# Two graph layers on one core: the transform back in small pieces behind given instructions, GpSimd's sums in order of use, and the next group's first layers 0 at a group's end

## The chip, the core and the metric

The kernel runs on one core of a Trainium2 chip. The metric is the time of one execution in microseconds (us) on the device. The engines are TensorE (PE: matmuls; PEld is its loading of weights), VectorE (DVE), ScalarE (ACT), GpSimd (POOL) and SyncE (SP), which here only issues transfers. Each takes its own instructions in a fixed order, and waits where one of them needs another engine or a transfer. All data is float32.

## What is computed

64 graphs of 256 nodes with 256 features go through two layers. Cut to what matters:

```
# layer 0
norm_adj = d_inv_sqrt[:, :, None] * adjacency_matrix * d_inv_sqrt[:, None, :]
h = einsum('bnm,bmf->bnf', norm_adj + alpha * eye(N), x)
x = layernorm(x + h @ W.T + b)
# layer 1
h = relu(bn1(conv1(x)))                      # per node
x_conv = relu(bn2(conv2(h)) + x)             # 17 taps along the nodes
s = x @ w_se.T + b_se                        # 3 numbers a node
A = exp(-dist(s, s)) * mask                  # mask: ones
x_nmp = A @ relu(x @ w_msg.T + b_msg)
gi = concat([x_conv, x_nmp]) @ w_ih.T + b_ih
gh = x @ w_hh.T + b_hh
# r, z = sigmoid of thirds of gi + gh, nn = tanh(gi_n + r * gh_n)
x = layernorm(x + (1 - z) * nn + z * x)
```

## The kernel before, in words

**Groups and passes.** The convolution of 17 taps is done in the frequency domain: each graph's 256 nodes are cut into 8 tiles of 32, and the spectra of 16 graphs fill the 128 rows of a matmul. So the 64 graphs form 4 groups of Q = 16, and there is one pass q of the transform for each group. A pass has four kinds of work:

- **Layers**: `layer0(g)` (L326) and `layer1(g, V, place)` (L403) for each graph. Layer 1 writes the graph's spectrum into the big tile V (L460), and stores what the gate needs (x1_d, xn_d) to DRAM.
- **Products**: 12 steps (`products`, L528) multiply the spectra by the taps' spectra u, which come from DRAM in 71 loads of 256 KB a pass on SP's queue (`load_u`, L498, six buffers). The results go into M, which is the same memory as V.
- **The transform back**, on DVE alone, in place in M: `real_transform` and `complex_begin` run with the steps, `complex_end` (L692) after them. `output` (L679) makes two of the 32 nodes of each tile and stores them to xc_d on SP's queue.
- **Gates**: `gru(g)` (L767) for each graph of the group. It reads inputs (the transposed features), and four sums of them that GpSimd makes (`input_sums`, L758) for a Strassen-like product with 7 blocks instead of 8. xc is read from DRAM, x1 is added to it by a transfer of GpSimd's queue (`residual`, L737), and it is transposed on PE (`transposed`, L743).

**How passes overlap.** V and M are one tile, so the next group's layers can't write V while the transform back still reads M. The first AHEAD = 6 graphs of the next group write a second tile V2 instead, and four ACT copies (L998) move them to V when the transform has ended. The other 10 graphs follow, with the first EARLY = 4 gates of the group just transformed beside them. The other 12 gates ("late") run beside the next pass. The pools of the gate tiles (`gate`) and of V2 (`ahead`) are opened once, before pass 0.

**How the order is made.** Each function is a generator; a `yield` ends a piece. The program from L966 on weaves pieces: `take(stage, n)` runs n pieces, `merge(main, other, every)` puts one piece of other behind every so many of main, `chain` joins stages, `graphs` (L879) runs layer 1 of a graph with layer 0 of the graph two further on at the places of `PLACES`. The order written so is a priority, not yet the order on an engine. A planner that models the durations places the instructions of every engine: of those that it holds to be ready, it takes the one that was written first. So an instruction can be moved far ahead of its place in the text where its inputs are ready early and its engine is idle in the model. `tc.issue_after(i)` in a `with` forbids this: instructions of the block on i's engine are placed behind i. It adds no wait of its own. On the chip the order on each engine is then fixed.

**Names and lines of the changed places.** Instructions on DVE, most of which read what PE has just made: x1 in layer 0 (L396), h (L423), msg (L444), aT (L481, which reads what ACT made) in layer 1, and first (L793), trz (L800), gn (L822), y (L840) in a gate. GpSimd's sums: S[:,2] is L761, S[:,0] L762, S[:,1] L763, S[:,3] L764. S[:,0] and S[:,3] read the transposed convolution; S[:,2] reads only what the transfers of `load_gate` bring; S[:,1] reads S[:,0]. In a gate the blocks with S[:,0] and S[:,1] come first (p15, p26), those with S[:,2] and S[:,3] after them (p7, p34). The layer norm's power is taken on GpSimd too (L308), as is that of the degrees (L352).

Of the kernel before, what the change touches and what calls it, by code (L numbers as in the profile page):

```python
# [26 lines left out]
def kernel(  # L27
# [55 lines left out]
    def accbank(name):  # L83
        return psacc.tile([P, 512], F32, tag="acc", name=name)


# [242 lines left out]
    def layer0(g):  # L329
# [65 lines left out]
        for c in range(NCH):  # L395
            nc.vector.scalar_tensor_tensor(  # L396
                x1[:, c, :], p[:, c, :], dis[:, c : c + 1], x_t[:, c, :], op0=ALU.mult, op1=ALU.add
            )
# [4 lines left out]
    def layer1(g, V, place):  # L403
# [13 lines left out]
        for c in range(NCH):  # L417
            p = bank("p_conv1")[:, : D + NSE]
            for k in range(DCH):
                nc.tensor.matmul(  # L420
                    p, x1T[:, k, c * P : (c + 1) * P], wc1[:, k, :], start=k == 0, stop=k == DCH - 1
                )
            nc.vector.tensor_tensor(h[:, c, :], p, bc1, op=ALU.add)  # L423
        nc.scalar.activation(h[:, :, :D], h[:, :, :D], AF.Relu)  # L424
# [14 lines left out]
        for c in range(NCH):  # L439
            for k in range(DCH):  # L440
                nc.tensor.matmul(  # L441
                    p[:, c, :], x1T[:, k, c * P : (c + 1) * P], wmsg[:, k, :], start=k == 0, stop=k == DCH - 1
                )
        nc.vector.tensor_tensor(msg, p, bmsg_t.unsqueeze(1).to_broadcast([P, NCH, D]), op=ALU.add)  # L444
        nc.scalar.activation(msg, msg, AF.Relu)
# [30 lines left out]
        for c in range(NCH):  # L476
# [3 lines left out]
            nc.scalar.activation(aT[:, c].rearrange("p n q -> p (n q)"), p, AF.Exp, bias=nsq[:, c : c + 1], scale=2.0)  # L480
        nc.vector.tensor_mul(aT, aT, adjT[:, :, 0:3:2, :])  # L481
        yield
# [90 lines left out]
    def four(re, im):  # L573


        by = im - re
        sub2(blocks(re, by, 2), blocks(re + 2, by, 2))
        sub2(blocks(re, by), blocks(re + 1, by))
        add2(M[:, re + 2, :], M[:, im + 3, :])
        sub2(M[:, im + 2, :], M[:, re + 3, :])  # L580

# [30 lines left out]
    def real_transform():  # L612
# [12 lines left out]

        four(8, 12)
        yield
# [30 lines left out]
    def four_turned(re, im, angle):  # L658


        by, low = abs(re - im), min(re, im)
        z = [blocks(low + i, by) for i in range(4)]
        c2, t2 = turned(re + 2, im + 2, 2 * angle)
        stt(z[2], t2, -c2, z[0], op0=ALU.mult, op1=ALU.add)
        stt(z[0], t2, c2, z[0], op0=ALU.mult, op1=ALU.add)
        yield
        c1, t1 = turned(re + 1, im + 1, angle)
        c3, t3 = turned(re + 3, im + 3, 3 * angle)
        stt(z[3], t3, -c3 / c1, t1, op0=ALU.mult, op1=ALU.add)
        stt(t1, t3, c3 / c1, t1, op0=ALU.mult, op1=ALU.add)  # L670
        stt(z[1], t1, -c1, z[0], op0=ALU.mult, op1=ALU.add)
        stt(z[0], t1, c1, z[0], op0=ALU.mult, op1=ALU.add)
        yield
        for lo, hi, by in ((re + 2, im + 3, c1), (im + 2, re + 3, -c1)):
            stt(M[:, hi, :], M[:, hi, :], by, M[:, lo, :], op0=ALU.mult, op1=ALU.add)
            stt(M[:, lo, :], M[:, lo, :], 2.0, M[:, hi, :], op0=ALU.mult, op1=ALU.subtract)
        yield

    def output(q, n, re, im):  # L679


        plain = M[:, n // 8 * 8 + ORDER.index(n % 8), :]
        x, y = M[:, re, :], M[:, im, :]
        t = freq.tile([P, 2, D], F32, name="turn", bufs=3)
        by = [real_part(t[:, j, :], x, y, 2 * math.pi * (n + 16 * j) / FL) for j in range(2)]
        low = min(re, im)
        for j in range(2):
            stt(M[:, low + 16 * j, :], t[:, j, :], by[j], plain, op0=ALU.mult, op1=ALU.add)
        nc.sync.dma_start(
            xc_d[q].rearrange("g (t a b) d -> (g t) a b d", a=2, b=16)[:, :, n, :], M[:, low : low + 17 : 16, :]  # L690
        )

    def complex_end(q):

        four(CR, CI)
        yield
        for outs in (((0, 0, 0), (8, 1, 0)), ((4, 2, 0), (12, 3, 1))):
            for n, i, exchanged in outs:
                output(q, n, (CR, CI)[exchanged] + i, (CI, CR)[exchanged] + i)
            yield  # L700

        add2(M[:, CR + 4 : CR + 6, :], M[:, CI + 6 : CI + 8, :])
        sub2(M[:, CI + 4 : CI + 6, :], M[:, CR + 6 : CR + 8, :])
        yield
        for n, re, im, angle in ((2, CR + 4, CI + 4, math.pi / 4), (6, CI + 6, CR + 6, 3 * math.pi / 4)):
            low = min(re, im)
            c, t = turned(re + 1, im + 1, angle)
            stt(blocks(low + 1, 16), t, -c, blocks(low, 16), op0=ALU.mult, op1=ALU.add)
            stt(blocks(low, 16), t, c, blocks(low, 16), op0=ALU.mult, op1=ALU.add)
            yield  # L710
            output(q, n, re, im)
            output(q, n + 8, re + 1, im + 1)
            yield
        for n, re, im, angle in ((1, CR + 8, CI + 8, math.pi / 8), (3, CI + 12, CR + 12, 3 * math.pi / 8)):
            yield from four_turned(re, im, angle)
            output(q, n, re, im)
            output(q, n + 8, re + 1, im + 1)
            yield
            output(q, n + 4, re + 2, im + 2)
            output(q, n + 12, im + 3, re + 3)  # L720
            yield

# [35 lines left out]
    def input_sums(g):  # L758
        A11, A12, A21, A22 = halves(GATE[g][1])
        S = SUMS[g] = gate.tile([P, 4, HALF, P], F32, name="sums", bufs=1)  # L760
        nc.gpsimd.tensor_tensor(S[:, 2], A11, A21, op=ALU.subtract)  # L761
        nc.gpsimd.tensor_tensor(S[:, 0], A21, A22, op=ALU.add)  # L762
        nc.gpsimd.tensor_tensor(S[:, 1], S[:, 0], A11, op=ALU.subtract)  # L763
        nc.gpsimd.tensor_tensor(S[:, 3], A12, S[:, 1], op=ALU.subtract)  # L764

    def gru(g):
# [25 lines left out]
        first = gate.tile([P, 2, D], F32, name="first", tag="gn")  # L792
        nc.vector.tensor_add(first, half(p15), brz_t)  # L793
        nc.vector.tensor_add(trz[:, 0:2], first[:, 0:1].to_broadcast([P, 2, D]), half(p26))
# [4 lines left out]
        nc.vector.tensor_add(trz[:, 3], trz[:, 1], p7[:, :D])  # L799
        nc.vector.tensor_add(trz[:, 1:3], trz[:, 1:4:2], half(p34))  # L800

# [6 lines left out]
        for c in range(NCH):  # L808
# [12 lines left out]
            gn = gate.tile([P, 2, D], F32, name="gn")  # L821
            nc.vector.tensor_add(gn, p.rearrange("p (i d) -> p i d", i=2), bn_t)  # L822
            nc.vector.scalar_tensor_tensor(
# [15 lines left out]
            y, t, n = x1[:, part], trz[:, 1:4:2][:, part], nn[:, part]  # L839
            nc.vector.scalar_tensor_tensor(y, t, 3.0, y, op0=ALU.add, op1=ALU.mult)  # L840
            nc.vector.scalar_tensor_tensor(n, t, 1.0, n, op0=ALU.subtract, op1=ALU.mult)
# [30 lines left out]
    def run(stage):  # L872
        for _ in stage:
            pass


    PLACES = (("other",), ("layer0",), (), (), ("layer0",), ("other", "layer0"), ())

    def graphs(first, part, V, others):  # L879


        for i in part:
            load(first + i + 3)
            given = {"layer0": layer0(first + i + 2) if i + 2 < Q else iter(()), "other": others[i]}
            for piece, _ in enumerate(layer1(first + i, V, i)):
# [49 lines left out]
    ustream = ctx.enter_context(tc.tile_pool(name="ustream", bufs=6))  # L935
    gate = ctx.enter_context(tc.tile_pool(name="gate", bufs=2))
    ahead = ctx.enter_context(tc.tile_pool(name="ahead", bufs=1))


    AHEAD = 6  # L940
    V2 = ahead.tile([P, FL, DCH, AHEAD * GT], F32, name="V2")
    EARLY = 4

# [16 lines left out]
    def nothing():  # L960
        return iter(())

    late = nothing()
    for q in range(NQ):
# [3 lines left out]
        if more:  # L968
            if q:
                others = [both(take(late, 3 if i % 3 == 0 else 2), take(end, 2)) for i in range(AHEAD)]  # L970
            else:
                others = [nothing() for _ in range(AHEAD)]
            begin = chain(merge(layer0(first), layer0(first + 1)), graphs(first, range(AHEAD), V2, others))
        sums(0)
        real = real_transform()
        for step in range(STEPS):
# [5 lines left out]
            if q:  # L982
                run(take(late, (0, 1, 1, 1, 1, 1, 2, 1, 2, 1, 2, 1)[step]))
            else:
                run(take(begin, 2 + step // 4))
        run(real)
        if not q:
            run(merge(begin, end, 3))
        elif more:
            run(merge(merge(take(late, 20), take(begin, 6), 3), take(end, 5), 5))  # L990
            run(begin)
        else:
            run(merge(late, end, 2))
        if more:
            run(late)
            run(end)
            for f in range(0, FL, 12):
                nc.scalar.copy(V[:, f : f + 12, :, : AHEAD * GT], V2[:, f : f + 12])  # L998
            early = gates(q, range(EARLY))
            others = [take(early, 2) for _ in range(Q)]  # L1000
            run(graphs(first, range(AHEAD, Q), V, others))
            run(early)
            late = gates(q, range(EARLY, Q))
        else:
# [54 lines left out]
```

## Time and profile before

| | us |
|---|---|
| three runs | 2186.56, 2187.06, 2191.32 |
| profiled execution | 2186.0 |
| PE busy | 2067.5 (95%) |
| DVE busy | 1547.1 (71%) |
| ACT busy | 831.2 (38%) |
| POOL busy | 664.5 (30%) |

The stages follow each other so: layers of group 0 with the making of the taps' spectra up to about 288 us; pass 0's products from there to about 400 us, its transform back to 470 us; then layers of group 1 with gates to 640 us. Pass 1's products run to 760 us and its transform back ends at 884 us; layers with gates go on to 1160 us. Pass 2 does the same 520 us later. Pass 3's products start at 1680 us and its transform back ends at 1926 us; what is left are gates alone.

In the profile's view of 40 slices each digit is the busy share of an engine in a slice of 54.6 us, in tenths. PE's time while it waits between matmuls counts as idle, but the end of a matmul is modelled, so counts of matmuls in a stretch say more than busy time.

### The profile page before, as it was taken

What the parts mean: (1) busy time and instruction counts of PE and PEld (TensorE: products, weight loads), DVE (VectorE), ACT (ScalarE), POOL (GpSimd) and SP (SyncE); (2) the same over time, 40 slices, a digit from 0 to 9 for tenths busy, and PEclk for the clock granted to TensorE, in tenths of its full rate; (3) what the DMA queues carried; (4) which work ended last, traced back from release to release, by engine and by line L of the source; (5) the groups of instructions that cost most, each with busy time, mean ns of one, the idle gap of its engine ahead of it and who ended that gap; (6) DMA issues with size and microseconds to landing.
All of it is one profiled execution on the core that took longest, in us unless ns stands there. A gap on an engine that the chain in (4) does not pass through costs nothing.

```text
span 2186.0 us, 28897 instructions
## 1 busy us (share of the span) xinstructions
PE 2067.5 (95%) x9805; PEld 1750.7 (80%) x9805; DVE 1547.1 (71%) x3691; ACT 831.2 (38%) x1847; POOL 664.5 (30%) x640
## 2 busy tenths in 40 slices
PE   6999899969999988999999998899999999899998
PEld 5888778758888876888888887788888887778887
DVE  5555458875568799655557889855565879987766
ACT  3665533445531123455452122446543112222222
POOL 2445310122322233223231224322231223344442
PEclk9999999989999999999999999999999999999999
DMA  3765656443346644434336654433334654344441
GB/s 110 239 193 194 222 178 207 151 134 102 111 137 201 191 130 108 131 91 123 105 101 190 207 144 130 116 114 108 102 97 126 205 160 118 114 121 111 105 113 53
DMA packets 251331, 305.64 MB, mean 140 GB/s; under 512 B 18324, under 2 KB 229864, under 8 KB 251184
## 3 DMA queue, kind: packets, MB, share of 16 engines
q1 hardware_dynamic: 183680, 200.46, 30.0%
q10 hardware_dynamic: 44480, 67.39, 8.7%
q0 software_dynamic: 23024, 35.95, 8.2%
q8 instruction: 78, 1.28, 0.2%
q14 instruction: 69, 0.57, 0.1%
HBM read 200.62 MB, written 103.06 MB: 139 GB/s over the span
## 4 chain that ended last, share of the span: by engine, by line
PE 50%; DVE 14%; issue 6%; POOL 6%; ACT 4%; DMA 0%; ACTq 0%; POOLq 0%; SPq 0%; DVEq 0%
PE p_rz L780 18%; PE p_n L817 9%; PE p_k L510 8%; PE p_nmp L486 2%; PE p_out L392 2%; PE p_dft L455 2%; PE p_conv L420 2%; POOL sums L762 2%; PE p_hT L382 1%; PE p_msg L441 1%; POOL ln_rs L308 1%; POOL sums L764 1%; PE p_dist L479 1%; POOL sums L763 1%; DVE gn L822 1%
## 5 line engine op out<-in xcount | busy, mean ns | idle before, releaser
L780 PE MATMUL p_rz<-wrz,sums 128*128 128x256 f32 x1536 | 355.8, 383 | 19.4 <-DVE gn L822 9.8
L817 PE MATMUL p_n<-wn,inputs 128*128 128x256 f32 x1536 | 353.0, 383 | 16.2 <-DVE first L793 15.7
L780 PEld LDWEIGHTS p_rz<-wrz,sums 128*128 128x128 f32 x1536 | 288.4, 191 | 70.7 <-issue 15.8
L817 PEld LDWEIGHTS p_n<-wn,inputs 128*128 128x128 f32 x1536 | 286.6, 191 | 62.6 <-DVE first L793 19.0
L780 PE MATMUL p_rz<-wrz,inputs 128*128 128x256 f32 x1152 | 272.9, 380 | 2.4 <-ACT inputs L752 1.8
L308 POOL TENSOR_TENSOR ln_rs<-ln_rs,neg_half 128x2 f32<-128x2 f32 x129 | 100.2, 777 | 537.3 <-DVE ln_rs L307 451.5
L780 PEld LDWEIGHTS p_rz<-wrz,inputs 128*128 128x128 f32 x1152 | 216.7, 190 | 33.9 <-ACT inputs L752 3.8
L352 POOL TENSOR_TENSOR dis<-deg,neg_half 128x2 f32<-128x2 f32 x64 | 48.6, 760 | 425.1 <-DVE deg L350 320.4
L829 ACT ACTIVATE nn<-gn 128x256 f32<-128x256 f32 x128 | 53.2, 416 | 326.0 <-DVE gn L826 325.5
L510 PE MATMUL p_k<-u,VM 128*128 128x256 f32 x736 | 175.1, 380 | 0.0
L318 ACT ACTIVATE x_g<-x_g,ln_mr,ln_rs 128x256 f32<-128x256 f32 x128 | 70.0, 593 | 256.4 <-DVE ln_mr L316 256.4
L510 PEld LDWEIGHTS p_k<-u,VM 128*128 128x128 f32 x736 | 138.6, 190 | 19.6 <-DMA u<-ud 0.7
L455 PE MATMUL p_dft<-fwd,h 128*128 128x240 f32 x512 | 121.4, 382 | 24.2 <-ACT h L424 23.1
L761 POOL TENSOR_TENSOR sums<-inputs 128x384 f32<-128x384 f32 x64 | 69.6, 1087 | 230.2 <-issue 172.3
L420 PE MATMUL p_conv<-wc,xn 128*128 128x259 f32 x512 | 127.4, 391 | 12.1 <-ACT xn L412 12.1
L455 PEld LDWEIGHTS p_dft<-fwd,h 128*128 128x128 f32 x512 | 98.2, 196 | 41.2 <-ACT h L424 32.9
L382 PE MATMUL p_hT<-adjT,x 128*128 128x256 f32 x512 | 126.8, 392 | 2.2 <-ACT adjT L362 1.5
L486 PE MATMUL p_nmp<-aT,msg 128*128 128x256 f32 x512 | 123.6, 385 | 2.6 <-DVE aT L481 2.6
L375 POOL TENSOR_TENSOR x_t<-x_t,b_t 128x512 f32<-128x512 f32 x64 | 84.8, 1325 | 134.5 <-ACT x L374 94.0
L392 PE MATMUL p_out<-w,hT 128*128 128x256 f32 x512 | 122.8, 382 | 1.1 <-ACT hT L387 0.9
L441 PE MATMUL p_msg<-wmsg,xn 128*128 128x256 f32 x512 | 122.1, 381 | 0.0
L420 PEld LDWEIGHTS p_conv<-wc,xn 128*128 128x128 f32 x512 | 96.8, 192 | 31.5 <-ACT xn L412 17.3
(154 smaller groups left out, 3838.6 us busy)
## 6 DMA issues: line engine op xcount, KB each, us to landing
u<-ud SPq DMA_DIRECT2D x284, 256.0 KB
xn_d<-xn ACTq DMA_DIRECT2D x64, 512.0 KB
inputs<-xn_d SPq DMA_DIRECT2D x64, 512.0 KB
ud<-u_set POOLq DMA_DIRECT2D x39, 480.0 KB, 6.1
adj_t<-in_adj_dram SPq DMA_DIRECT2D x64, 256.0 KB
x_t<-in_x_dram SPq DMA_DIRECT2D x64, 256.0 KB
x_d<-x ACTq DMA_DIRECT2D x64, 256.0 KB
x_g<-x_d SPq DMA_DIRECT2D x64, 256.0 KB
```

What stands on the lines that cost most here:

```text
L308: nc.gpsimd.tensor_tensor(rs[:, : len(chunks)], rs[:, : len(chunks)], neg_half[:, : len(chunks)], op=ALU.pow)
L318: nc.scalar.activation(y[:, c, :], y[:, c, :], AF.Identity, bias=mr[:, c : c + 1], scale=rs[:, c : c + 1])
L375: nc.gpsimd.tensor_tensor(x_t, x_t, b0_t.unsqueeze(1).to_broadcast([P, NCH, D]), op=ALU.add)
L382: nc.tensor.matmul(p[:, k, :], x1[:, mc, k * P : (k + 1) * P], adjT[:, mc, 1 - mc : 3 - mc, :].rearrange("p n q -> p (n q)"), start=mc == ...
L392: nc.tensor.matmul(p[:, c, :], hT[:, k, c * P : (c + 1) * P], w0[:, k, :], start=k == 0, stop=k == DCH - 1)
L420: nc.tensor.matmul(p, x1T[:, k, c * P : (c + 1) * P], wc1[:, k, :], start=k == 0, stop=k == DCH - 1)
L441: nc.tensor.matmul(p[:, c, :], x1T[:, k, c * P : (c + 1) * P], wmsg[:, k, :], start=k == 0, stop=k == DCH - 1)
L455: nc.tensor.matmul(p[:, t0 * FL : t1 * FL], h[:, c, k * P : (k + 1) * P], fwd[:, first : first + t1 - t0, :].rearrange("p t f -> p (t f)") ...
L486: nc.tensor.matmul(p[:, k, :], msg[:, mc, k * P : (k + 1) * P], aT[:, mc].rearrange("p n q -> p (n q)"), start=mc == 0, stop=mc == NCH - 1,)
L510: nc.tensor.matmul(p[:, j * D : (j + 1) * D], v[:, k, :], u[:, k, :], start=k == 0, stop=k == DCH - 1)
L780: nc.tensor.matmul(p[:, j * D : (j + 1) * D], a[:, k], wrz[:, b, k], start=k == 0, stop=k == HALF - 1)
L817: nc.tensor.matmul(p[:, o * D : (o + 1) * D], lhsT, w, start=j == 0, stop=j == len(part) - 1)
```

## The change

It has five parts.

1. `complex_end` and what it calls get more `yield`s: 58 pieces in place of 18 (`four` in `real_transform` is run whole).
2. The eight kinds of DVE instructions named above are noted as `marks`. A new function `paced(main, other, rate)` runs main, and behind each mark it places `rate` pieces of other on average, each under `issue_after` of that mark. The ends of the four passes use it with rates 1.2, 0.85, 0.85 and 1.35, in place of `merge` and of pieces in `others`. In pass 3 six gate pieces run with the steps in place of 14.
3. GpSimd's sums are written S[:,0], S[:,1], S[:,2], S[:,3], and the last two are placed behind the second.
4. `graphs` runs layer 0 of the graph two further on also for the last two graphs of a group, so the next group's first two layers 0 come at a group's end and no longer at its start.
5. In pass 0 AHEAD is 12: V2 is twice as large, and closed behind its copies; only then the gate pool is opened, and a V2 for 6 graphs after the early gates. The first four gates run 5 pieces to a graph beside 4 graphs, in place of 2 pieces beside 10. In pass 0 every step takes 3 pieces of layers (before: 2, 2, 2, 2, 3, 3, 3, 3, 4, 4, 4, 4).

```diff
+    marks = []
+    def mark(op):
+        marks.append(op.ins)
...
-            nc.vector.tensor_tensor(h[:, c, :], p, bc1, op=ALU.add)
+            mark(nc.vector.tensor_tensor(h[:, c, :], p, bc1, op=ALU.add))
...
     def complex_end(q):
-        four(CR, CI)
-        yield
-        for outs in (((0, 0, 0), (8, 1, 0)), ((4, 2, 0), (12, 3, 1))):
-            for n, i, exchanged in outs:
-                output(q, n, (CR, CI)[exchanged] + i, (CI, CR)[exchanged] + i)
-            yield
+        yield from four(CR, CI)
+        yield
+        for n, i, exchanged in ((0, 0, 0), (8, 1, 0), (4, 2, 0), (12, 3, 1)):
+            yield from output(q, n, (CR, CI)[exchanged] + i, (CI, CR)[exchanged] + i)
...
-        nc.gpsimd.tensor_tensor(S[:, 2], A11, A21, op=ALU.subtract)
         nc.gpsimd.tensor_tensor(S[:, 0], A21, A22, op=ALU.add)
-        nc.gpsimd.tensor_tensor(S[:, 1], S[:, 0], A11, op=ALU.subtract)
-        nc.gpsimd.tensor_tensor(S[:, 3], A12, S[:, 1], op=ALU.subtract)
+        second = nc.gpsimd.tensor_tensor(S[:, 1], S[:, 0], A11, op=ALU.subtract)
+
+        with tc.issue_after(second.ins):
+            nc.gpsimd.tensor_tensor(S[:, 2], A11, A21, op=ALU.subtract)
+            nc.gpsimd.tensor_tensor(S[:, 3], A12, S[:, 1], op=ALU.subtract)
...
+    def paced(main, other, rate):
+        marks.clear()
+        due = 0
+        for _ in main:
+            for i in marks:
+                due += rate
+                while due >= 1:
+                    due -= 1
+                    with tc.issue_after(i):
+                        next(other, "end")
+            marks.clear()
+            yield
...
-            given = {"layer0": layer0(first + i + 2) if i + 2 < Q else iter(()), "other": others[i]}
+            given = {"layer0": layer0(first + i + 2) if first + i + 2 < B else iter(()), "other": others[i]}
...
-                others = [both(take(late, 3 if i % 3 == 0 else 2), take(end, 2)) for i in range(AHEAD)]
+                others = [take(late, 3 if i % 3 == 0 else 2) for i in range(AHEAD)]
...
-            begin = chain(merge(layer0(first), layer0(first + 1)), graphs(first, range(AHEAD), V2, others))
+            begin = graphs(first, range(AHEAD), V2, others)
...
-                run(take(late, (0, 1, 1, 1, 1, 1, 2, 1, 2, 1, 2, 1)[step]))
+                run(take(late, (0, 1, 1, 1, 1, 1, 2, 1, 2, 1, 2, 1)[step] if more else step % 2))
             else:
-                run(take(begin, 2 + step // 4))
+                run(take(begin, 3))
         run(real)
         if not q:
-            run(merge(begin, end, 3))
+            run(paced(begin, end, RATES[q]))
         elif more:
-            run(merge(merge(take(late, 20), take(begin, 6), 3), take(end, 5), 5))
-            run(begin)
+            run(paced(chain(merge(take(late, 20), take(begin, 6), 3), begin), end, RATES[q]))
         else:
-            run(merge(late, end, 2))
+            run(paced(late, end, RATES[q]))
+            run(end)
...
                 nc.scalar.copy(V[:, f : f + 12, :, : AHEAD * GT], V2[:, f : f + 12])
-            early = gates(q, range(EARLY))
-            others = [take(early, 2) for _ in range(Q)]
+            if q == 0:
+                scope.close()
+                gate = ctx.enter_context(tc.tile_pool(name="gate", bufs=2))
+            early = gates(q, range(EARLY))
+            others = [take(early, 5 if q == 0 else 2) for _ in range(Q)]
             run(graphs(first, range(AHEAD, Q), V, others))
             run(early)
+            if q == 0:
+                scope, AHEAD, V2 = open_ahead(6)
+                ctx.enter_context(scope)
```

## The prediction

> **What bounds the kernel now.** I read four views: the page's slices, the busy times by stretch, the waits of the TensorE (PE), and the timelines around the longest waits. The slices say where. PE is at 9 almost everywhere, and the three dips lie where VectorE (DVE) shows its 8s and 9s, not where it is idle:
>
> ```profile
> PE   6999899969999988999999998899999999899998
> DVE  5555458875568799655557889855565879987766
> ```
>
> The busy times by stretch give sizes (columns: the stretch in us, its length, then busy us and instruction count of PE, PE's weight loads, DVE, ACT, POOL, then granted clock, DMA share, GB/s):
>
> ```profile
> 240.00:300.00 60.00, 49.97 (x220) 39.24 (x219) 23.71 (x70) 25.97 (x61) 12.41 (x12) 0.89 0.49 160
> ...
> 400.00:480.00 80.00, 58.36 (x265) 45.44 (x264) 71.52 (x208) 36.96 (x82) 16.47 (x15) 0.89 0.42 130
> ...
> 640.00:760.00 120.00, 120.00 (x565) 105.45 (x564) 96.73 (x184) 21.62 (x43) 25.14 (x23) 1.00 0.70 211
> 760.00:900.00 140.00, 124.91 (x574) 104.87 (x573) 129.70 (x299) 44.26 (x97) 52.40 (x46) 0.96 0.45 123
> 900.00:1160.00 260.00, 256.48 (x1265) 216.81 (x1264) 148.20 (x405) 136.24 (x309) 73.72 (x76) 1.00 0.35 104
> ...
> 1280.00:1420.00 140.00, 124.98 (x567) 103.82 (x566) 128.21 (x297) 44.27 (x97) 51.87 (x46) 0.96 0.44 122
> ...
> 1800.00:1960.00 160.00, 141.84 (x649) 118.33 (x648) 149.21 (x307) 37.10 (x76) 62.72 (x55) 1.00 0.43 118
> 1960.00:2160.00 200.00, 200.00 (x956) 176.10 (x955) 140.10 (x273) 52.38 (x110) 83.33 (x81) 1.00 0.41 105
> ```
>
> Read the counts, not PE's busy time: a matmul that is kept waiting or runs at half clock looks busier. The last stretch, gates alone, takes 956 matmuls in 200 us, 209 ns each; 900 to 1160, layers with gates, 206 ns. At that rate 574 matmuls are 119 us, so 760:900 lost 21 us; 1280:1420 (567) lost 22 us; 1800:1960 (649 at 209) lost 24 us. In pure layers (62 matmuls in 12.0 us by the start-to-start times, 216 ns a full one and 109 ns a transpose: 194 ns) 400:480 lost 80 - 51 = 29 us. 240:300 (197 ns, a mix) lost 17 us. DVE is 93% busy in the middle two and the fourth, 89% in the first, and 57% and 70% right behind them. So the four ends of the transform back are **DVE-bound**, in a kernel that is PE-bound elsewhere. The two longest waits of PE in 400:480 show how:
>
> ```profile
> 461.61 3.57 PE L455 MATMUL p_dft<-fwd,h 128*128 128x240 f32 x8 [9.56 <-ACT h L424]
> 470.44 0.69 PE L468 MATMUL p_rows<-ident,scols 128*128 128x128 f32 x2 [5.25 <-DVE scols L433]
> ```
>
> DVE adds h (L423) at 459.5 and 460.5 only; from 450 to 459 it runs transform instructions queued ahead. The 17 us before 300 are something else: GpSimd took a gate's first sum (L761), not needed before 400 us, and stood at its transfer, with the layer norm's power queued behind:
>
> ```profile
> 265.45 0.99 POOL L761 TENSOR_TENSOR sums<-inputs 128x384 f32<-128x384 f32 x1 [10.88 <-DMA x_g<-x_d]
> 266.40 0.71 POOL L352 TENSOR_TENSOR dis<-deg,neg_half 128x2 f32<-128x2 f32 x1
> 267.07 0.71 POOL L308 TENSOR_TENSOR ln_rs<-ln_rs,neg_half 128x2 f32<-128x2 f32 x1
> ```
>
> **What the Trainium skill says.** "TensorE: Matmul & The Clock Gate", section "Architectural detail": ACT, DVE and GpSimd queues are strict FIFO. The two timelines agree. The same page, "What's actually happening": after an idle window of about 3.4 us PE's clock is halved. The trace agrees: behind the 9.56 us wait 8 matmuls took 3.57 us, against 1.89 us for the same 8 at 251.97. "Perfetto Trace Analysis", "Optimization Strategy": where the most-contended engine changes over time, interleave the regimes. That is the case here. "SBUF — State Buffer", "SBUF: two separate sides": GpSimd and a DVE instruction with two SBUF inputs exclude each other. It agrees: the 128x512 turn L708 took 1.69 us once against 0.69 us; so I count DVE as full at 97%.
>
> **The parts.** Units first. A gate is 66 matmuls of 216 ns and 4 transposes, 14.7 us of PE; its DVE is 140.1/200 x 14.7 = 10.3 us. A graph's layers are 12.0 us of PE; 900:1160 is graphs with half a gate each (19.4 us of PE), DVE 57% of that, 11.2, less 5.1: 6.1 us. The end of the transform, from its listed instructions at back-to-back steps of 0.34 (256 wide), 0.60 (512) and 1.14 us (1024): 16 outputs x 4 x 0.34 = 21.4, first four 4.8, sums 2.4, two turns 3.8, two four-turns 13.9: **46 us** of DVE a pass, in 58 pieces after the change, 0.80 us each.
>
> 1. *Pinned pieces.* No DVE work is removed; it is spread. Passes 1 and 2 (0.85 a mark): a gate has 5 marks, 4.25 pieces, 3.4 us, DVE 13.7 of 14.7 us (93%); a graph 6 marks, 4.1 + 6.1 of 12.0 us (85%). 58 pieces need 68 marks, and 34 pieces of gates (42 marks) with 6 graphs (36) give 78. Both are below 97%: PE sets the pace; with DVE at 81% (96.7 of 120) 640:760 lost nothing, so at up to 93% I leave 4 us of latencies each, of 21 and 22: gain 35 (bounds 20 and 43). Behind a mark that waits for PE the pieces wait too, and the next add behind them; the tightest is `first`, whose bank p_n takes 3.9 us (18 matmuls) later, against pieces of 0.3 to 2.3 us: it holds.
> 2. *Pass 0* (1.2): 36 of 120 pieces run in the steps as before; 84, 8.4 graphs with 50 marks, take 58 pieces in 48. DVE 7.2 x 0.8 + 6.1 = 11.9 of 12.0 us a graph, 99%: over 97%, about 3 us short in 8 graphs, plus latencies and a burst at the close. Before it was 46 us of pieces against some 3 graphs. I take a loss of 11 for 29: gain 18 (bounds 5 and 26).
> 3. *Pass 3* (1.35): 8 gate pieces leave the steps. From the first product on: 284 products of 216 ns, 61 us, with 10.1 gates 210 us of PE; DVE 61 (96.7 in 1680:1800 less 3.5 gates) + 46 + 104 = 211 us, as much as PE. A gate with its 6.75 pieces is 15.7 us on DVE against 14.7. Also the u loads (71 of 256 KB, 18.6 MB in some 83 us, 224 GB/s; 0.70 of the engines carried 211) come close to starving products. Loss 14 for 24: gain 10 (bounds -4 and 18).
> 4. *Layer 0 at a group's end.* 2 x 3.9 us of PE moves from the next pass into 240:300; sum unchanged, it fills idle PE. Its loads are in place (x_t at 261), its stores go to ACT's queue, which idled 6.7 us there.
> 5. *GpSimd's order.* Four sums remain, 4.4 us a gate. S[:,0] needs the transposed convolution, so none can be taken early; S[:,1] was behind three and is behind two, but it waits for ACT's inputs, so in steady gates (no PE loss in 1960:2160) it is worth nothing, while S[:,2] and S[:,3] come 1 us later and are needed 5 us later. Also the gate pool does not exist before pass 0's end, so no load of it is early. With 4: 17 us become 5, gain 12; the later group ends, about 2 us each, give 2.
> 6. *12 graphs ahead, the gate pool afterwards.* The four copies of V2 (L998, 1.15 us) double: 4.6 us more of ACT (at 52% in that stretch). Gate 0's loads on SP's queue then stand behind the copies: copies 9, loads 5, residual 4.9, transposes and sums 5, 24 us, beside 48 us of layers of the last four graphs. Between 0 (hidden) and 24 lost; I take 3.
>
> Sum: 35 + 18 + 10 + 12 + 2 - 3 = 74 us from the profiled execution's 2186, so 2112; the timed runs (2186.6 to 2191.3, median 2187.1) stand 1 us above it: **2113**.
>
> **Rivals.**
> A. The above: PE-bound again in passes 1 and 2, DVE still a little short in 0 and 3. 2085 to 2140. Chance 0.63.
> B. The pins only say "not before": pieces queue up behind marks that come late in bursts, DVE stays saturated locally. For it: DVE at 99% in passes 0 and 3, 0.6 us of DVE idle at each wait for ln_rs. Then half of the end losses stay, and part 6 costs 8: 96/2 + 12 - 8 = 52 at best, 21 + 12 - 8 = 25 if passes 0 and 3 give nothing: 2135 to 2162, about 2150. Chance 0.17.
> C. All four ends and the group end vanish: 21 + 22 + 29 + 24 + 17 = 113: 2073. Against it: 99%. Chance 0.12.
> D. Slower: each pinned piece sits in front of an add that frees a PSUM bank, in 8 graphs, 2 x (8.5 gates + 4.5 graphs) and 8.6 gates, 43 units. It decides once DVE's backlog passes the 3.9 us of `first`; the whole chain of each unit then moves. At 3 us a unit it costs 129 us against 113 won at most: 2186 - 113 + 129 = 2202. Against it: 93% and 85% leave DVE time to catch up in two passes. Chance 0.07.
> The remaining 0.01 is no change at all.
>
> **Range and chances.** 0.2% (4.4 us) is about what a measurement of this kernel tells from no change. Range 2075 to 2150: A, most of C and the better half of B. Faster 0.91, same 0.02, slower 0.07.
>
> **What would show it.** In the profile of the changed kernel: DVE at 85 to 95% in long stretches instead of 57% behind 97%; the waits of p_dft for h, of p_n for `first` and of p_rz for gn (23.1, 15.7 and 9.8 us now) together under 15; no sum on GpSimd in group 0; the clock without dips between 240 and 2160. I am wrong if PE still loses over 15 us in pass 1 or 2, if the steps of pass 3 wait for u, or if PE stands over 10 us ahead of gate 0.

## The result and the profile after

The changed kernel takes **2173.7 us** (median of four runs, 2171.0 to 2175.6) against 2187.9 (2186.6 to 2191.3): a ratio of 0.9932, 95% interval 0.9915 to 0.9949. It is 14 us faster, where 74 were forecast; the measured time lies above the range that was given.

The view of 40 slices (54.2 us each) shows PE's dip in pass 0 shallower but wider than before: it now takes slices 8 to 10, 380 to 542 us. The dips at group 0's end and in pass 1 are gone, of pass 2's two slices one is left, and pass 3's single 8 stands as before:

```profile
PE   6999999887999999999999999899999998999998
DVE  5555568785568798775556989775555889977776
```

The busy times by stretch, columns as in the prediction; 389:520 is pass 0's end, and 520:560 what follows on it:

```profile
240.00:300.00 60.00, 57.50 (x280) 47.55 (x280) 35.00 (x99) 32.20 (x76) 14.94 (x15) 1.00 0.57 181
...
389.00:520.00 131.00, 113.22 (x547) 89.70 (x545) 105.10 (x306) 72.79 (x166) 25.61 (x26) 1.00 0.37 119
520.00:560.00 40.00, 30.61 (x135) 25.41 (x136) 12.19 (x35) 18.68 (x35) 18.13 (x17) 0.87 0.57 155
760.00:900.00 140.00, 132.03 (x625) 113.16 (x624) 122.88 (x274) 45.17 (x98) 52.85 (x48) 0.98 0.41 116
900.00:1160.00 260.00, 253.70 (x1240) 212.39 (x1240) 157.53 (x431) 134.51 (x309) 74.08 (x76) 1.00 0.37 109
...
1800.00:1960.00 160.00, 149.60 (x692) 128.16 (x691) 142.16 (x294) 38.45 (x81) 66.74 (x60) 0.99 0.46 120
```

240:300 has 280 matmuls for 220: the group's end is filled. 760:900 has 625 for 574. But 900:1160 has 1240 for 1265, and 389:520 has only 547 in 131 us, with DVE at 80%: PE waits there although DVE is not full. The waits of PE that the prediction named did shrink: p_dft for h from 23.1 to 12.1 us, p_n for `first` from 15.7 to 10.6, p_rz for gn from 9.8 to 0.8. Others grew: p_dist for dist_r from 7.5 to 16.9 us, p_conv for the copy of x1T (xn) from 12.1 to 17.6.

To compare kernels stage by stage I take PE's **loss**: the length of a stretch less the matmuls that start in it, each at its start-to-start time when nothing is waited for (216 ns for a 256-wide one, 109 a transpose, and so on; the work sums to 2001.2 us in both kernels). Stages are bounded by the first and last product of a pass. us lost:

| | to pass 0's products | pass 0, behind its products | pass 1, likewise | pass 2, likewise | pass 3, to its gates | products | last gates |
|---|---|---|---|---|---|---|---|
| before | 52.6 | 35.1 | 30.8 | 30.8 | 24.1 | 2.2 | 9.2 |
| after | 39.3 | 43.4 | 25.6 | 24.7 | 17.2 | 8.2 | 9.6 |

So 13.3 us were won at the start, 5.2, 6.1 and 6.9 in passes 1 to 3; 8.3 were lost in pass 0 and 6 in the products. With 0.4 lost in the last gates that is 16.8, the difference of the two profiled executions (2186.0 and 2169.2).

Part of the first column is chance. In the first 100 us all kernels of this document run the same instructions in the same order on PE, DVE, ACT and GpSimd, and their profiles still lose between 29.0 and 34.6 us there. For a group's end I therefore also give the loss from 240 us to the first product: 17.0 before, 4.7 after.

### The profile page after: what moved, and what is told of

Same layout as the page of the kernel before. It is cut to its first block, busy times and chain, and to the rows that moved or that the text cites. A ratio compares the mean times of both kernels' runs of the same rounds, so it can differ in the third digit from the quotient of the medians.

```text
span 2169.2 us, 29039 instructions
## 1 busy us (share of the span) xinstructions
PE 2062.6 (95%) x9805; PEld 1746.3 (81%) x9805; DVE 1551.3 (72%) x3691; ACT 833.2 (38%) x1847; POOL 664.0 (31%) x640
## 5 line engine op out<-in xcount | busy, mean ns | idle before, releaser
L833 PE MATMUL p_n<-wn,inputs 128*128 128x256 f32 x1536 | 356.0, 385 | 10.8 <-DVE first L809 10.6
L796 PE MATMUL p_rz<-wrz,sums 128*128 128x256 f32 x1536 | 350.9, 382 | 3.2 <-POOL sums L775 2.3
L775 POOL TENSOR_TENSOR sums<-inputs 128x384 f32<-128x384 f32 x64 | 67.8, 1059 | 334.3 <-ACT inputs L766 319.9
L518 PEld LDWEIGHTS p_k<-u,VM 128*128 128x128 f32 x736 | 138.0, 190 | 24.3 <-DMA u<-ud 2.0
L428 PE MATMUL p_conv<-wc,xn 128*128 128x259 f32 x512 | 127.9, 392 | 17.6 <-ACT xn L420 17.6
L463 PE MATMUL p_dft<-fwd,h 128*128 128x240 f32 x512 | 117.7, 373 | 13.3 <-ACT h L432 12.1
L489 DVE TENSOR_TENSOR aT<-aT,adjT 128x512 f32<-128x512 f32 x64 | 44.3, 692 | 110.9 <-ACT aT L488 110.9
```

The costliest lines, as they stand in the source:

```text
L428: nc.tensor.matmul(p, x1T[:, k, c * P : (c + 1) * P], wc1[:, k, :], start=k == 0, stop=k == DCH - 1)
L463: nc.tensor.matmul(p[:, t0 * FL : t1 * FL], h[:, c, k * P : (k + 1) * P], fwd[:, first : first + t1 - t0, :].rearrange("p t f -> p (t f)") ...
L518: nc.tensor.matmul(p[:, j * D : (j + 1) * D], v[:, k, :], u[:, k, :], start=k == 0, stop=k == DCH - 1)
L796: nc.tensor.matmul(p[:, j * D : (j + 1) * D], a[:, k], wrz[:, b, k], start=k == 0, stop=k == HALF - 1)
L833: nc.tensor.matmul(p[:, o * D : (o + 1) * D], lhsT, w, start=j == 0, stop=j == len(part) - 1)
```

## The experiments

Times are medians; each run's ratio is to the kernel before on the same chip.

**1. Six graphs ahead** (part 5 undone, and the transform back of pass 0 woven without pins).

```diff
-    scope, AHEAD, V2 = open_ahead(12)
+    gate = ctx.enter_context(tc.tile_pool(name="gate", bufs=2))
+    ahead = ctx.enter_context(tc.tile_pool(name="ahead", bufs=1))
+    AHEAD = 6
+    V2 = ahead.tile([P, FL, DCH, AHEAD * GT], F32, name="V2")
...
-            run(paced(begin, end, RATES[q]))
+            run(merge(begin, end, 1))
```

> The changed kernel with its fifth part undone: 6 graphs ahead in pass 0, the gate pool open from the start, the early gates 2 pieces to a graph, and pass 0's end woven without pins (one piece of the transform behind each layer piece). Theory 1 (the gain was given back in pass 0: layers alone leave gaps, and the doubled V2 copies hold ACT; the stretch 300 to 640 us lost 47 us of PE against 37 before): 10 us come back, about 2163. Theory 2 (it was the pins that cost, pass 0's form is neutral): within 4 us of the changed kernel, 2170 to 2178.

2170.7 us, ratio 0.9933 (0.9913 to 0.9953): not told from the changed kernel. Pass 0 lost 43.0 us, as much as with 12. So part 5 is not worse than what it replaced here, but also no better; theory 1 is wrong as it was put. In this run the loss sits in one place (440 to 460 us lost 18.8), since only 2.4 graphs are left to weave with: 24 of the 58 pieces stand behind a piece of layers, and the rest follow in a row.

**2. No pins.**

```diff
-                    with tc.issue_after(i):
-                        next(other, "end")
+                    next(other, "end")
```

> The changed kernel with every piece written at the same place but without issue_after, so the planner may take it as early as its inputs allow. Theory 1 (the pins spread the work; they are what passes 1, 2 and 3 gained, about 9, 10 and 5 us): 2174 + 24 and something in pass 0, about 2195 to 2205, with DVE full again in the first part of each end. Theory 2 (the pins put pieces in front of adds that PE waits for and cost as much as they save): 2165 to 2176.

2189.6 us, ratio 1.0016 (1.0006 to 1.0025). Passes 1 and 2 lost 35.6 and 33.4 us, against 25.6 and 24.7 with pins; pass 3 19.8 against 17.2. So the pins are worth 10, 9 and 3 us there, and without them the whole change is no gain. That is theory 1, but the time lies 5 us below its range, since pass 0 lost 38.9 us, 4.5 less than with pins. Its busy times show DVE packed again into the first part, as before the change:

```profile
760.00:900.00 140.00, 123.09 (x566) 103.53 (x566) 129.30 (x286) 40.38 (x88) 57.12 (x46) 0.96 0.42 117
900.00:1160.00 260.00, 255.14 (x1254) 214.92 (x1253) 145.50 (x404) 135.03 (x306) 73.66 (x77) 1.00 0.35 106
```

**3. The sums in the old order**, in the changed kernel, and **4. the new order alone**, in the kernel before (the same edit the other way round).

```diff
+        nc.gpsimd.tensor_tensor(S[:, 2], A11, A21, op=ALU.subtract)
         nc.gpsimd.tensor_tensor(S[:, 0], A21, A22, op=ALU.add)
-        second = nc.gpsimd.tensor_tensor(S[:, 1], S[:, 0], A11, op=ALU.subtract)
-
-        with tc.issue_after(second.ins):
-            nc.gpsimd.tensor_tensor(S[:, 2], A11, A21, op=ALU.subtract)
-            nc.gpsimd.tensor_tensor(S[:, 3], A12, S[:, 1], op=ALU.subtract)
+        nc.gpsimd.tensor_tensor(S[:, 1], S[:, 0], A11, op=ALU.subtract)
+        nc.gpsimd.tensor_tensor(S[:, 3], A12, S[:, 1], op=ALU.subtract)
```

> The changed kernel with GpSimd's sums in the old order. Behind the ends of passes 1 and 2, where nothing is pinned, the changed kernel loses 5 us more a pass than before (8.7 against 3.9 in 940 to 1140). Theory 1 (the new order of the sums moves gates and layers against each other there): 10 us come back, about 2164. Theory 2 (it is the place of layers 0, or the sums matter nowhere once the gate pool opens late): 2172 to 2177.

> The kernel before with the new order of the sums alone. All theories: no sum can stand on GpSimd at 255 to 265 us, so the 5 us wait of p_dft there goes and the end of group 0 loses some 6 to 10 us less. Theory 1: 10 us of it are given back behind the ends of passes 1 and 2, about 2186. Theory 2: nothing is given back, 2177 to 2181.

2161.5 us (0.9884, 0.9869 to 0.9899) with the old order, 12 us faster than the changed kernel; 2192.3 us (1.0025, 1.0013 to 1.0036) with the new order alone, slower than before although the group's end lost 8.6 us less. Passes 1 and 2 lost 19.8 and 19.2 us in the first (25.6 and 24.7 changed) and 36.4 and 33.1 in the second (30.8 before). So theory 1 holds in both runs, and more was given back in the second than it forecast (2186): its pass 0 lost 6 us more than the kernel before as well. **In the changed kernel the new order costs 5 to 6 us in each of passes 1 and 2**; alone it costs 5.6 and 2.3 there. In pass 3 it wins some 2 us (17.2 lost, some 19 with the old order). The timelines of GpSimd (columns: start, duration, instruction, idle time before it) show why. The changed kernel, in a stretch where nothing is pinned:

```profile
1060.15 1.00 POOL L775 TENSOR_TENSOR sums<-inputs 128x384 f32<-128x384 f32 x1 [2.53 <-ACT inputs L766]
1061.23 1.00 POOL L776 TENSOR_TENSOR sums<-sums,inputs 128x384 f32<-128x384 f32 x1
1062.19 1.45 POOL L779 TENSOR_TENSOR sums<-inputs 128x384 f32<-128x384 f32 x1
1063.60 0.99 POOL L780 TENSOR_TENSOR sums<-inputs,sums 128x384 f32<-128x384 f32 x1
1064.54 1.24 POOL L753 DMA_DIRECT2D xc_g<-x_d  x1
1065.34 1.18 POOL L314 TENSOR_TENSOR ln_rs<-ln_rs,neg_half 128x2 f32<-128x2 f32 x1
```

and the run with the old order, where S[:,2] (L775) has run while GpSimd would have waited for ACT's inputs:

```profile
1055.89 1.00 POOL L775 TENSOR_TENSOR sums<-inputs 128x384 f32<-128x384 f32 x1
1058.40 1.00 POOL L776 TENSOR_TENSOR sums<-inputs 128x384 f32<-128x384 f32 x1 [1.50 <-ACT inputs L766]
1059.48 1.00 POOL L777 TENSOR_TENSOR sums<-sums,inputs 128x384 f32<-128x384 f32 x1
1060.56 1.33 POOL L778 TENSOR_TENSOR sums<-inputs,sums 128x384 f32<-128x384 f32 x1
1061.83 1.25 POOL L753 DMA_DIRECT2D xc_g<-x_d  x1
1062.63 1.20 POOL L314 TENSOR_TENSOR ln_rs<-ln_rs,neg_half 128x2 f32<-128x2 f32 x1
```

Four sums and a transfer's issue now stand in a row ahead of the layer norm's power, instead of three. DVE stands at ln_mr until that power is there, and h, for which PE's p_dft waits, is queued behind ln_mr. Of the changed kernel, DVE and then PE:

```profile
1066.55 0.16 DVE L322 SCALAR_TENSOR_TENSOR ln_mr<-ln_mv,ln_rs 128x2 f32<-128x2 f32 x1 [2.89 <-POOL ln_rs L314]
1069.68 1.89 PE L463 MATMUL p_dft<-fwd,h 128*128 128x240 f32 x8 [0.65 <-ACT h L432]
```

With the old order DVE's wait is 1.95 us, and PE has none there. From 940 us to pass 2's products PE waits for h six times in the changed kernel, 3.4 us in all, and twice in run 3, 0.8 us. That is 2.6 of the 4.6 us of loss by which the two differ in this stretch (10.4 and 5.8); the rest is not traced to single waits.

**5. Layers 0 at a group's end alone**, in the kernel before.

```diff
-            given = {"layer0": layer0(first + i + 2) if i + 2 < Q else iter(()), "other": others[i]}
+            given = {"layer0": layer0(first + i + 2) if first + i + 2 < B else iter(()), "other": others[i]}
...
-            begin = chain(merge(layer0(first), layer0(first + 1)), graphs(first, range(AHEAD), V2, others))
+            begin = graphs(first, range(AHEAD), V2, others)
```

> The kernel before with layers 0 of the next group at a group's end, and nothing else. The sums alone took 8.6 us off the loss ahead of pass 0 (52.6 to 44.0 us), both and the rest 13.3. If layer 0 fills PE's idle time at the group's end by itself: 4 to 6 us faster, about 2181. Rival: the early sum that stands on GpSimd holds layer 0's own powers too, so nothing is gained while it is there: 2185 to 2190.

2187.5 us, ratio 0.9998 (0.9989 to 1.0006): no change. The number is the rival's, its reason is not. The early sum was still there and stood 10.5 us, and yet the group's end was filled: from 240 us to the first product 10.7 us were lost in place of 17.0. (The whole start lost 3.7 us less, 48.9; its first 100 us lost 2.3 more by chance.) What was won there went elsewhere: pass 0 lost 4.0 more (39.1 against 35.1), the products some 2 more.

**6. Pass 0 without the end of its transform.**

```diff
+        if q == 0:
+            for low, n in enumerate((0, 8, 4, 12, 2, 10, 6, 14, 1, 9, 5, 13, 3, 11, 7, 15), CR):
+                yield
+                yield
+                nc.sync.dma_start(...)
+                yield
+            return
         yield from four(CR, CI)
```

> The changed kernel whose pass 0 leaves out the end of the transform back: its 58 pieces become 16 stores of M as it stands and no DVE work (46 us of DVE less). It tells what pass 0's layers lose by themselves. Theory 1 (layers without gates beside them lose PE time by their own chain of x1T, conv, dist, whatever DVE has to do): of the 24 us lost in 389 to 520, 15 or more stay; 2160 to 2168. Theory 2 (the pinned pieces delay the adds): 5 us or less stay; 2145 to 2155.

The kernel leaves out 46 us of DVE work in pass 0 and stores M as it stands. 2157.8 us, of a single run. Of the 19.3 us that PE lost from 400 to 500 us, **12.2 stay** with DVE busy 49.2 us of the 100. The work that took the changed kernel 131 us (389:520, 547 matmuls) takes 121 us here, of which 16 are lost:

```profile
400.00:500.00 100.00, 93.20 (x453) 75.65 (x454) 49.20 (x154) 58.96 (x139) 19.30 (x23) 1.00 0.31 103
389.00:510.00 121.00, 111.92 (x545) 90.40 (x543) 63.01 (x188) 73.12 (x162) 21.70 (x25) 1.00 0.32 105
```

So both theories hold a part, theory 1 the larger. Layers alone take 13.65 us a graph here, x1T to x1T (440.32 to 453.98 below), with 12.0 us of matmuls and transposes in them; with the pinned pieces it is 14.6 (444.11 to 458.72 in the changed kernel). Without the transform:

```profile
440.32 0.60 PE L419 MATMUL p_x1T<-ident,x 128*128 128x128 f32 x4
441.65 2.02 PE L428 MATMUL p_conv<-wc,xn 128*128 128x259 f32 x8 [0.73 <-ACT xn L420]
...
453.98 0.60 PE L419 MATMUL p_x1T<-ident,x 128*128 128x128 f32 x4
```

and with it, in the changed kernel:

```profile
444.11 0.60 PE L419 MATMUL p_x1T<-ident,x 128*128 128x128 f32 x4
445.43 2.02 PE L428 MATMUL p_conv<-wc,xn 128*128 128x259 f32 x8 [0.73 <-ACT xn L420]
...
454.53 0.70 PE L487 MATMUL p_dist<-dist_r,dist_l 32*128 32x256 f32 x4 [0.84 <-DVE dist_r L480]
...
458.72 0.60 PE L419 MATMUL p_x1T<-ident,x 128*128 128x128 f32 x4
```

The conv must wait for x1T to be copied by ACT in both, and there is no gate whose matmuls PE could do meanwhile. The pieces add waits, here for dist_r, in the next graph for adjT too (0.83 us).

**7. Pass 0's copies of V2 in 16 parts**, and later **10. written one by one behind the pieces of graph 28** (in the kernel of run 3). Of the first, and of the second:

```diff
-            for f in range(0, FL, 12):
-                nc.scalar.copy(V[:, f : f + 12, :, : AHEAD * GT], V2[:, f : f + 12])
+            by = 12 if q else 3
+            for f in range(0, FL, by):
+                nc.scalar.copy(V[:, f : f + by, :, : AHEAD * GT], V2[:, f : f + by])
```

```diff
+            by = 12 if q else 4
+
+            def copies():
+                for f in range(0, FL, by):
+                    nc.scalar.copy(V[:, f : f + by, :, : AHEAD * GT], V2[:, f : f + by])
+                    yield
+
+            if q:
+                run(copies())
+            else:
+                run(merge(graphs(first, range(AHEAD, AHEAD + 1), V, [nothing() for _ in range(Q)]), copies()))
...
-            others = [take(early, 5 if q == 0 else 2) for _ in range(Q)]
-            run(graphs(first, range(AHEAD, Q), V, others))
+            others = [take(early, 7 if q == 0 else 2) for _ in range(Q)]
+            run(graphs(first, range(AHEAD + (q == 0), Q), V, others))
```

> The changed kernel with pass 0's four copies of V2 (2.1 us each on ACT) cut into 16 of 3 frequencies. If x1T's 7.6 us wait and the half clock behind it come from the size of a copy, ACT takes other work between: 5 to 8 us faster than the changed kernel, 2166 to 2169. Rival: the copies are written first and are taken first whatever their size, so they stand as one block: 2172 to 2176.

> The changed kernel with the sums in the old order (2161 us) and pass 0's copies of V2 cut into 12 and written one behind each piece of graph 28, whose layers then run ahead of the gate pool's opening. Theory 1 (it is the copies' place at the head of ACT's queue that makes x1T wait 7 us and halves the clock): 6 to 10 us faster, 2151 to 2155. Rival (the wait only moves to the gates' first loads, which now come 10 us later): 2159 to 2165.

Small copies: 2173.2 us (0.9929, 0.9914 to 0.9944), no change; the rival. Woven copies: **2155.3 us** (0.9854, 0.9840 to 0.9869), 6 us faster than run 3; theory 1. Pass 0 lost 35 us in it, as much as in the kernel before, against 43 in run 3. In the changed kernel ACT's last two copies stand ahead of the one that PE waits for, and behind that wait PE is at half speed (8 conv matmuls in 3.60 us, 2.02 elsewhere; granted clock 0.50 from 527 to 529 us). ACT, then PE, in the changed kernel:

```profile
522.47 4.12 ACT L1032 COPY VM<-V 128x2304 f32<-128x2304 f32 x2 [0.58 <-ACT x L324]
526.50 0.58 ACT L420 COPY xn<-p_x1T 128x512 f32<-128x512 f32 x1
```

```profile
518.90 0.60 PE L419 MATMUL p_x1T<-ident,x 128*128 128x128 f32 x4
527.13 3.60 PE L428 MATMUL p_conv<-wc,xn 128*128 128x259 f32 x8 [7.63 <-ACT xn L420]
```

The same matmuls took 3.82 us behind a wait of 7.10 in the run with small copies, and 3.82 behind 7.17 in run 3. In the run with woven copies:

```profile
523.02 3.11 PE L428 MATMUL p_conv<-wc,xn 128*128 128x259 f32 x8 [4.00 <-ACT xn L420]
```

It is the place in ACT's queue that costs, not the size: the 16 small ones were taken in three rows, the last of seven. This wait and the matmuls behind it account for some 4 of the 6 us; run 10 also runs graph 28 without a gate beside it and weaves the four early gates with three graphs instead of four, and what that did was not measured apart.

**8. Six graphs ahead, S[:,2] held**: run 1 with the old order of the sums, and S[:,2] under `issue_after` of its graph's residual transfer.

```diff
+        with tc.issue_after(RESIDUAL[g]):
+            nc.gpsimd.tensor_tensor(S[:, 2], A11, A21, op=ALU.subtract)
         nc.gpsimd.tensor_tensor(S[:, 0], A21, A22, op=ALU.add)
...
```

> Six graphs ahead in pass 0 and no pins there (as in the run of that name), and the sums in the old order, but S[:,2] held behind the issue of the same graph's residual transfer on GpSimd. Theory 1 (the new order costs 5 to 6 us in each of passes 0, 1 and 2 because four sums and a transfer stand in a row ahead of the layer norm's power; the early sum is kept away all the same): 2171 - 16 = 2152 to 2158. Rival (holding S[:,2] puts it back into the row): 2167 to 2173.

2159.0 us (0.9864, 0.9847 to 0.9880). Passes 1 and 2 lost 20.1 and 19.7 us, as in run 3: once more 5 us each from the sums, theory 1; in pass 0 only 2 of its 5 to 6 us came (40.9 against 43.0), so the time lies 1 us above its range. Both numbers of graphs ahead stand within 3 us again (2161.5 with 12).

**9. The same, woven as coarsely as before** in pass 0.

```diff
-            run(merge(begin, end, 1))
+            run(merge(begin, chunks(end, 3), 3))
```

> The run with six graphs ahead and S[:,2] held (2159 us), with pass 0's transform woven as coarsely as before the change (three pieces behind every third layer piece). Pass 0's end lost 40.9 us there and 35.1 in the kernel before. If the fine weave without pins is what cost these 6 us: 2152 to 2155. Rival: the difference comes from layers 0 having moved to the group's end, out of pass 0 (39.1 in the run with that alone): 2157 to 2161.

2158.0 us (0.9868, 0.9852 to 0.9884), no different from run 8. Pass 0 lost 39.1 us, exactly as in run 5. So the fine weave accounts for some 2 of the 6 us at most; the 4 us that stay fit the place of layers 0, the rival.

**11. Pass 0 without pins, in the kernel of run 10.**

```diff
-                    with tc.issue_after(i):
+                    with tc.issue_after(i) if rate != RATES[0] else ExitStack():
```

> The same with the pins of pass 0 off and those of passes 1 to 3 kept. In the run without any pins pass 0's end lost 38.9 us against 43.4. If pins cost in pass 0, where only layers run (they hold back work that DVE could do in its gaps), 4 us faster than the run with woven copies. Rival (without pins the transform fills DVE first and delays the adds): 3 to 8 us slower than it.

2155.6 us (0.9857, 0.9841 to 0.9873), the same as run 10; pass 0 lost 36.0 us against 35.1. Neither theory: with the copies woven, pins in pass 0 cost nothing and bring nothing that the times show.

The best is run 10: the change with the old order of the sums and the copies woven, 2155.3 us, 18 us faster than the changed kernel.

## Why the prediction was wrong

Four steps failed: that PE sets the pace where DVE's sum is below 97%, so that only "4 us of latencies each" are left in passes 1 and 2 (15 were); "a loss of 11" in pass 0 (25); 3 us for what stands behind the copies there (13 more than before); and that the new order of the sums "is worth nothing" (it cost 5 to 6 us in each of passes 1 and 2). Of the 57 us between 74 and the 16.8 of the profiled executions, 26 are missing in passes 1 and 2, 23 in pass 0, 5 in pass 3 and 4 in the products of the other passes; the start gave 1 more than forecast.

*What bounds the kernel.* Right in the place: the four ends and the group's end are where both kernels lose. The reading of the slices was loose: where PE dips lowest (437 to 492 us) DVE's digit is 7, and at the group's end it is 4. Wrong in the inference behind all sizes, that PE sets the pace wherever DVE's sum stays below 97%. Run 6 refutes it: DVE busy half the time and PE still loses 12 of 100 us.

*Part 1, passes 1 and 2* (gain 35, bounds 20 and 43). The mechanism is right: the pins win 10 and 9 us (run 2). The size failed in one term, "I leave 4 us of latencies each". Over the stretches that I counted (752 to 940 and 1272 to 1440 before) the loss went from 24.3 and 25.6 to 15.3 and 15.4, so the term is 15 (14 and 13 with the old order of the sums), and the gain 19. A third or more of it is one event (4.8 us of waiting and the half clock behind it), in pass 1 here and in pass 2 again at 1367.91: the narrow copy dist_r stands in DVE's queue behind a gate's gn and two pieces, and PE has p_dist ahead of the gate's other matmuls. The changed kernel's DVE, and its PE:

```profile
849.71 1.21 DVE L839 SCALAR_TENSOR_TENSOR gn<-trz,gn 128x256 f32<-128x256 f32 x1
850.84 1.21 DVE L704 SCALAR_TENSOR_TENSOR VM<-turn,VM 128x256 f32<-128x256 f32 x1
851.97 0.41 DVE L842 SCALAR_TENSOR_TENSOR gn<-gn 128x256 f32<-128x256 f32 x1
852.41 0.43 DVE L480 COPY dist_r<-p_rows 64x256 f32<-64x256 f32 x1
```

```profile
852.90 1.22 PE L487 MATMUL p_dist<-dist_r,dist_l 32*128 32x256 f32 x4 [4.80 <-DVE dist_r L480]
```

I had checked the slack of `first` alone (it held: PE waited 0.2 us for it in this stretch); the short chain is that of the layers. The rest of the 15 us was not taken apart.

*Part 2, pass 0* (gain 18, bounds 5 and 26), and *part 6* (a loss of 3, bounds 0 and 24). Together they were to win 15, and pass 0 lost 8.3 more than before. Up to the copies it lost 25 us (389 to 520), where the kernel before lost 29 to 30 (up to 480): a gain of 4 to 5, at the lower bound. The step that failed is the same criterion, "DVE 11.9 of 12.0 us a graph, ... about 3 us short". What it left out is what layers lose by themselves where no gate runs beside them, as in these graphs: 13.65 us a graph before any piece (16 of the 25 us stay without DVE's pieces, run 6), 14.6 with pieces. Behind that it lost 18 us, against 5.5 before; 13.5 of them from 520 to 560 us. That is within part 6's bounds by luck rather than by its reason. Some 9 are ACT's queue, whose 4.6 us more I had set beside 52% of busy time: the 7.63 us wait for x1T and the slow matmuls behind it. Gate 0's loads, the reason given, hold the other 4 or so: GpSimd stood 2.54 us at the transfer of the next gate's xc ahead of the sums, PE then 1.84 us at the sums (547.24), and 24 matmuls behind it took 7.13 us, which is 5.2 at 216 ns each. Run 10 won the 8 us of the whole pass back.

*Part 3, pass 3* (gain 10, bounds -4 and 18). 24.1 became 17.2, less 2.1 in its products: 4.8 us. Inside the bounds, but not all by its reason: pins are worth 3 of it, and some 2 come from the sums' order, which the forecast had put at nothing. The slack of `first`, called safe, was not safe here: PE waited 10.2 us for it, 7.2 before. The loads of u held PE for 3.1 us in the whole kernel and, as the profile has it, not at all in pass 3's steps: that fear did not come true.

*Parts 4 and 5 at group 0's end* (17 become 5, gain 12). From 240 us to the first product 17.0 became 4.7. Right, with its cause: no sum stands there any more. The sums alone leave 8.6 there (run 4), layers 0 alone 10.7 (run 5). The new order was not needed for it, though. With the old order in the changed kernel, where the gate pool opens late, 4.9 are left (run 3), and with S[:,2] pinned also 4.9 (run 8). The 2 us at the later group ends did not come, and run 5's other half, that layer 0 was taken from pass 0 and costs 4 us there, was no part of my sum: I had "sum unchanged".

*Part 5 elsewhere*: "in steady gates ... it is worth nothing". For the last gates that is so (9.2 and 9.6 us in the last stage). The step failed because I asked only who waits for S[:,2] and S[:,3], not what is queued behind them on GpSimd. That costs 5 to 6 us in each of passes 1 and 2 (12 us in run 3's time), the largest error after pass 0 and the latencies of part 1.

*The rivals and the signs.* Case B comes nearest, but not by its mechanism: the pins hold their pieces, and DVE is not saturated. D's mechanism, a pinned piece ahead of what PE needs, is not settled: the pieces cost about 1 us a graph in pass 0 (14.6 less 13.65), a third of its price, but whether by their pins is open, since without pins pass 0 lost 4.5 us less in run 2 and 1 us more in run 11. Of the signs of being right only one came true in full, that no sum runs on GpSimd in group 0. The three waits fell from 48.6 to 23.5 us, not under 15; DVE is at 88% in 760:900 but still at 61% behind it; the clock still dips. Of the signs of being wrong the first came (passes 1 and 2 lose 15 us at their ends and 25 in all), the second and third did not.

## What to carry to other kernels

An engine's busy share says whether it can be the bound by throughput; whether another engine waits for it is told by what stands ahead of the awaited instruction in its queue, so trace that chain for the stage as it will be, not for the stage it is now. Before moving an instruction on a shared engine, list what is queued behind its new place: here one sum of 1 us, which had run while GpSimd waited, was put into the row ahead of a layer norm's power, and that cost 11 us in two passes, more than the pins won in either. And work that fills another stage's gaps (gates beside layers, layers 0 at a pass's start) is not free to move: what it leaves has to be charged.

## What was not expected of the hardware

DVE instructions of 256 elements with two inputs in SBUF took 1.21 us instead of 0.41 (849.71 and 850.84 above) while GpSimd's sums ran:

```profile
849.47 1.17 POOL L779 TENSOR_TENSOR sums<-inputs 128x384 f32<-128x384 f32 x1
850.60 1.17 POOL L780 TENSOR_TENSOR sums<-inputs,sums 128x384 f32<-128x384 f32 x1
```

That fits the exclusion that the prediction cited, but at three times the duration; the allowance of 3% of DVE's time did not show what it does to one chain. PE's half clock came after shorter waits than the 7 to 9 us of the other examples: after 4.0 us (8 conv matmuls in 3.11 us instead of 2.02, run 10), after 4.8 us (4 p_dist in 1.22 instead of 0.70), and in one place of the changed kernel after waits of 0.37 and 1.84 us within 3 us (544.70 and 547.24; granted clock 0.57 from 547 to 551 us).
